# First cross attention of a perceiver block: mask conversion in pieces between rounds, value chunks ahead of key chunks, one copy of the queries in the scratch

## The chip, the cores and the metric

The kernel runs on one core of a Trainium2 chip. The metric is the device time of one execution in microseconds (us); lower is better. Times of before are the median of 3 runs.

## What is computed

The program is a block of six stages, each adding to `x` of shape (2, 256, 256): a cross attention, a convolution and gate layer, a quantised feed-forward layer, a second cross attention, a self attention with heads of 64, and a mixture of experts. The change lies in the first stage alone:

```
q = proj(layernorm(x), Wq, bq); k = proj(ctx, Wk, bk); v = proj(ctx, Wv, bv)   # 16 heads of 16
energy = einsum('bhqd,bhkd->bhqk', q, k) / sqrt(16)
energy = where(mask_input == 0, -1e9, energy)                                  # mask: 256 x 4096, int32
context = einsum('bhqk,bhkd->bhqd', softmax(energy), v)
x = x + context @ Wo.T + bo
```

`x` has 2 batches of 256 queries, `ctx` has 2 batches of 4096 keys of width 256. All is float32.

## The kernel before, in words

`l0_xattn` works through 16 units `u`, each a batch and a pair of heads. Keys are projected in chunks of 512 (`project_k(b, f, j, ct)`, L185: two matmuls for half `f` of the features, a bias on ACT into `kf`, a split into a high part on DVE and a low part on POOL, `split` L174, and two DMAs, L197, into a scratch in DRAM, `KS`). A unit's keys come back from the scratch in another layout (`load_k`, L211, into `kst`, 3 buffers), its queries likewise (`load_q`, L201, from `QS` into `qz`, 4 buffers). Both copies hold a high and a low part of each number, and the queries hold each of them twice. Values are projected in two halves per chunk (`project_v`, L334; a yield after each half), copied on ACT (L351), and stay on chip in `v`.

The main loop (L546) has 8 rounds `g` per unit and two passes `a` per round, one for each head of the pair. Three things run in it, shifted against one another: in unit `u` the scores `st` with queries on the partitions (L388), of which DVE takes the maximum with the mask added (`max_out`, L397, two `st` buffers); ten rounds later the scores `sT` with keys on the partitions and the maximum taken off (`weights_part`: L404 adds a mask with a matmul, L411 the maximum, L421 the scores; exp on ACT L427; POOL multiplies the other half's mask in, L429); and eleven rounds later the sum over values (`weigh`, L437).

So the mask is wanted in two forms. `madd` (queries on the partitions) is made by `make_madd(qc, j, mi)`, L247, one DVE operation for each of 8 pieces and each half `qc` of the queries. `addT` and `keep` (keys on the partitions, L323 and L325) are made from `x0_maskT` in 16 pieces by `make_masks`, which ends with two reductions over `madd` (L328). The raw masks go through the tile `mi` with 3 buffers; the first half's go into `keep`, which is free then.

Work that is not part of the rounds is written as generators in the list `slow`; each pass takes one step of each of them before its own work. `first_batch` gives the rest of the keys and the values of batch 0, `masks` the rest of the masks, `second_batch` (from round 14) the keys of batch 1, `second_values` (from round 68) its values, `project_out` (L460) the output projection of a batch when its last unit is done. Five steps of `first_batch` are taken ahead of the loop: values 0, keys 0 and values 1.

PE, DVE, ACT and POOL execute in the order in which the program writes the instructions (`tc.manual_schedule`, L1236). All DMAs are issued by SP, whose order the scheduler of the framework sets. An engine that waits holds everything behind it. The lines that set the order before the change are

```
for j in range(NJ):
    make_madd(0, j, mis[j])
...
early = first_batch()
for _ in range(5):
    next(early)
slow = [early, masks()]
```

Of the kernel before, what the change touches and what calls it, by code (L numbers as in the profile page):

```python
# [10 lines left out]
F32 = mybir.dt.float32  # L11
# [7 lines left out]
P = 128  # L19
B = 2  # L20
S = 256
NTOK = B * S
# [23 lines left out]
class Kernel:  # L46
# [96 lines left out]
    def l0_xattn(self):  # L143
        nc, T, tc = self.nc, self.T, self.tc
        H, HD, VD, NJ = 16, 16, 17, 8
# [4 lines left out]
        dram = es.enter_context(tc.tile_pool(name="scratch", bufs=1, space=bass.MemoryType.DRAM))  # L150
# [11 lines left out]


        KS = {(b, f): dram.tile([2, P, 2, S2 // 2], F32, name=f"ks{b}{f}") for b in range(B) for f in range(2)}
        QS = [dram.tile([P, 2, 2, NTOK], F32, name=f"qs{f}") for f in range(2)]

        def part_tile(n, early):
            if early:
# [16 lines left out]
        def project_k(b, f, j, ct):  # L185

            ps = self.bank("psK")
            for k in range(2):
                nc.tensor.matmul(  # L189
                    ps, lhsT=w[:, 0, k, f * P : (f + 1) * P], rhs=ct[:, k, :], start=k == 0, stop=k == 1  # L190
                )
            kf = a2.tile([P, 512], F32, name="kf", tag="kf")
            nc.scalar.activation(kf, ps, AF.Identity, bias=bk[:, f : f + 1])
            part = part_tile(512, b + f == 0)
            split(part[:, 0, :], part[:, 1, :], kf)
            for h in range(2):
                nc.sync.dma_start(KS[b, f][h, :, :, j * S : (j + 1) * S], part[:, :, h * S : (h + 1) * S])  # L197

        qz, kst = {}, {}

        def load_q(u):  # L201
            b, hp = divmod(u, NP)
            f, lp = divmod(hp, 4)
            qz[u] = a1.tile([P, 2, S], F32R, name="qz", tag="qz", bufs=4)
            for h in range(2):
                nc.sync.dma_start(
                    qz[u][64 * h : 64 * h + 64].bitcast(F32),
                    QS[f].rearrange("p j i n -> (p j) i n")[64 * lp : 64 * lp + 64, :, b * S : (b + 1) * S],
                )

        def load_k(u, c0, c1):  # L211
            b, hp = divmod(u, NP)
# [9 lines left out]
        cts = [load_ctx(0, 0), load_ctx(0, 1)]  # L222
# [14 lines left out]
        def load_mask(qc, j):  # L237

            mi = a2.tile([P, 2, S], I32, name="mi", tag="mi", bufs=3) if qc else keep[:, j]
            nc.sync.dma_start(  # L240
                mi.rearrange("p a b -> p (a b)"), T["x0_mask"][qc * P : (qc + 1) * P, j * 512 : (j + 1) * 512]
            )
            return mi

        def make_madd(qc, j, mi):
            c, a = divmod(j, 2)
            nc.vector.tensor_scalar(madd[:, qc, c, :, a], mi, 0, -BIG, ALU.is_equal, ALU.mult)  # L247

        mis = []
        self.layernorm(self.xn, self.x)  # L250
        for j in range(NJ):
            project_k(0, 0, j, cts[j])
            if j == 1:
                self.to_T(self.xnT, self.xn)
            if j == 2:
                for f in range(2):
                    ps = self.bank("psQ")
                    for k in range(2):
                        nc.tensor.matmul(
                            ps, lhsT=wq[:, k, f * P : (f + 1) * P], rhs=self.xnT[:, k, :], start=k == 0, stop=k == 1  # L260
                        )
                    qf = a2.tile([P, NTOK], F32, name="qf", tag="kf")

                    nc.vector.tensor_scalar(qf, ps, bq[:, f : f + 1], 0.25, ALU.add, ALU.mult)
                    part = part_tile(NTOK, True)
                    split(part[:, 0, :], part[:, 1, :], qf)
                    for i in range(2):
                        nc.sync.dma_start(QS[f][:, i], part)
            if j == 4:
                load_q(0)  # L270
            if j >= 4:
                mis += [load_mask(0, 2 * (j - 4)), load_mask(0, 2 * (j - 4) + 1)]
            if j in (3, 5, 7):
                load_k(0, j - 3, j - 1)
        load_k(0, 6, 8)
        for j in range(NJ):
            make_madd(0, j, mis[j])

        def rest_of_mask():
            ahead = [load_mask(1, 0), load_mask(1, 1)]  # L280
            for j in range(NJ):
                if j + 2 < NJ:
                    ahead.append(load_mask(1, j + 2))
                yield
                make_madd(1, j, ahead[j])

        bv = a1.tile([P, D], F32, name="bv")
        wo = a1.tile([P, 2, D], F32, name="wo")
# [45 lines left out]
        def project_v(b, j, ct):  # L334

            n = 4 * H * VD
            vf[b, j] = a1.tile([P, n + 16], F32, name="v", tag="v", bufs=9)
            v = vf[b, j][:, :n].rearrange("p (r h s) -> p r h s", r=4, h=H)
            nc.gpsimd.memset(v[:, :, :, HD:VD], 1.0)
            nc.gpsimd.memset(vf[b, j][:, n:], 0.0)  # L340
            for a in range(2):
                ps = self.bank("psV").rearrange("p (r e) -> p r e", r=2)
                for i in range(2):
                    for k in range(2):
                        n0 = (2 * a + i) * P
                        nc.tensor.matmul(  # L346
                            ps[:, i, :], lhsT=ct[:, k, n0 : n0 + P], rhs=w[:, 1, k, :], start=k == 0, stop=k == 1
                        )
                vo, vi = v[:, 2 * a : 2 * a + 2, :, 0:HD], ps.rearrange("p r (h s) -> p r h s", s=HD)
                if b == 0:  # L350
                    nc.scalar.copy(vo, vi)  # L351
                    sum_ctx(b, j, a, ct)
                else:
                    self.evac(vo, vi)
                yield
# [104 lines left out]
        def project_out(b, cxo):  # L460

            cm = self.sm.tile([P, 2], F32, name="cm", tag="cm")
            nc.vector.tensor_reduce(cm, csum[:, b], AX.X, ALU.add)
            nc.vector.tensor_scalar(cm, cm, 1.0 / S2, None, ALU.mult)
            ps = self.bank("psN")[:, 0:D]
            for k in range(2):
                nc.tensor.matmul(
                    ps, lhsT=cm[:, k : k + 1].to_broadcast([P, P]), rhs=w[:, 1, k, :], start=k == 0, stop=k == 1
                )
            mean = a2.tile([P, D], F32, name="mean", tag="mean", bufs=1)  # L470
            nc.scalar.copy(mean, ps)
            yield
            yield
            for qc in range(2):
                t = 2 * b + qc

                cf = cxo[:, qc].rearrange("p h s -> p (h s)")
                nc.vector.scalar_tensor_tensor(cf, mean, none[:, qc : qc + 1], cf, ALU.mult, ALU.add)
                nc.vector.tensor_tensor(cf, cf, bv, ALU.add)
                nc.vector.tensor_tensor(self.x[:, t, :], self.x[:, t, :], bo, ALU.add)  # L480
            yield
            for qc in range(2):
                t = 2 * b + qc
                cf = cxo[:, qc].rearrange("p h s -> p (h s)")
                ps = self.bank("psX")[:, 0:D]
                for k in range(2):
                    nc.tensor.transpose(ps[:, k * P : (k + 1) * P], cf[:, k * P : (k + 1) * P], self.ident)
                cT = a2.tile([P, 2, P], F32, name="cT", tag="cT")
                nc.scalar.copy(cT.rearrange("p a b -> p (a b)"), ps)
                yield  # L490
                yield
                ps = self.bank("psO")[:, 0:D]
                for k in range(2):
                    nc.tensor.matmul(ps, lhsT=cT[:, k, :], rhs=wo[:, k, :], start=k == 0, stop=k == 1)
                nc.vector.tensor_tensor(self.x[:, t, :], self.x[:, t, :], ps, ALU.add)
                yield
# [6 lines left out]
        def chain(gens):  # L503
            for g in gens:
                yield from g
# [4 lines left out]

        def first_batch():

            for j in range(NJ):
                yield from project_v(0, j, cts[j])
                project_k(0, 1, j, cts[j])
                yield

        def second_batch():
# [19 lines left out]
        def masks():  # L538
            yield from rest_of_mask()
            yield from make_masks()  # L540

        early = first_batch()
        for _ in range(5):
            next(early)
        slow = [early, masks()]
        for g in range(8 * NU + 12):  # L546
            u, i = divmod(g, 8)
# [14 lines left out]
            u2, j = divmod(g - 10, 8)  # L562
            u3, j3 = divmod(g - 11, 8)

            for a in range(2):
# [4 lines left out]
                if 0 <= u2 < NU:  # L570
                    p = pt[u2, j, a] = a2.tile([P, 2, 2, S], F32, name="p", tag="p", bufs=5)
                    part = weights_part(qz[u2], kst[u2], msh[u2], a, j, p)
# [766 lines left out]
```

## Time and profile before

| what | before |
|---|---|
| median of 3 runs | 1223.26 us (1222.86 to 1226.22) |
| the profiled execution | 1223.28 us |
| its span, first to last instruction | 1221.5 us |
| busy in the span: PE, DVE, ACT, POOL | 1058.0, 678.3, 461.0, 401.2 us |
| mean granted clock of PE | 0.912 |
| key and query scratch: DMAs L197, L268 | 64 of 256 KB, 4 of 512 KB |
| loads of queries L206, of keys L217 | 32 of 128 KB, 38 |
| last addition to `x` in the stage (L495) starts | 651.69 us |

All times in the stage are us from the first instruction. PE is the tensor engine's matmuls and PEld its weight loads; DVE, ACT and POOL are the vector, scalar and GpSimd engines; SP only issues DMAs. In a line of the timeline come the start, the duration, the engine, the source line, the operation, what it writes and reads, how often, and in square brackets how long the engine had been idle and what released it. In the chain of waits, each line is a piece of the chain that ended last. "Granted clock" is the share of its full clock that PE was given.

### The profile page before, as it was taken

What the parts mean: (1) busy time and instruction counts of PE and PEld (TensorE: products, weight loads), DVE (VectorE), ACT (ScalarE), POOL (GpSimd) and SP (SyncE); (2) the same over time, 40 slices, a digit from 0 to 9 for tenths busy, and PEclk for the clock granted to TensorE, in tenths of its full rate; (3) what the DMA queues carried; (4) which work ended last, traced back from release to release, by engine and by line L of the source; (5) the groups of instructions that cost most, each with busy time, mean ns of one, the idle gap of its engine ahead of it and who ended that gap; (6) DMA issues with size and microseconds to landing.
All of it is one profiled execution on the core that took longest, in us unless ns stands there. A gap on an engine that the chain in (4) does not pass through costs nothing.

```text
span 1221.5 us, 20524 instructions
## 1 busy us (share of the span) xinstructions
PE 1058.0 (87%) x8203; PEld 614.3 (50%) x8204; DVE 678.3 (56%) x1243; ACT 461.0 (38%) x926; POOL 401.2 (33%) x424
## 2 busy tenths in 40 slices
PE   6688899999999899999996595239799889888888
PEld 3354455555566555555553143124466663365666
DVE  3168666666754677777505916974344427557330
ACT  2334466666654456666651210210211212336010
POOL 4114577777763467777760000000000000000000
PEclk9788899999999999999996798558899989979879
DMA  9895044444222211221006623110336440000000
GB/s 320 257 272 176 33 116 113 131 113 117 58 62 70 44 45 46 45 45 36 2 1 226 229 69 99 52 38 27 92 115 194 150 138 0 1 1 1 1 1 18
DMA packets 54446, 108.54 MB, mean 89 GB/s; under 512 B 5568, under 2 KB 27968, under 8 KB 52432
## 3 DMA queue, kind: packets, MB, share of 16 engines
q1 hardware_dynamic: 54352, 107.24, 29.4%
q8 instruction: 64, 1.05, 0.4%
q14 instruction: 30, 0.25, 0.1%
HBM read 87.82 MB, written 19.40 MB: 88 GB/s over the span
## 4 chain that ended last, share of the span: by engine, by line
PE 78%; DVE 13%; issue 3%; ACT 3%; DMA 2%; POOL 1%; SPq 1%; POOLq 0%; ACTq 0%; DVEq 0%
PE av L437 12%; PE st L388 9%; PE sT L421 8%; PE psP L133 7%; PE sT L404 6%; PE psS L909 5%; PE psV L346 4%; PE psK L189 4%; PE av L930 4%; PE ot L1086 2%; DVE yb L687 2%; DVE nm L918 1%; PE psR L999 1%; PE psC L448 1%; PE psI L1209 1%
## 5 line engine op out<-in xcount | busy, mean ns | idle before, releaser
L397 DVE CUSTOM_DVE_ANT_0 junk<-st,madd 128x1024 bf16<-128x1024 f32 x256 | 313.2, 1223 | 113.8 <-PE st L388 112.5
L429 POOL TENSOR_TENSOR p<-p,keep 128x512 int32<-128x512 int32 x256 | 327.7, 1283 | 144.9 <-ACT p L427 138.0
L427 ACT ACTIVATE p<-sT 128x512 f32<-128x512 f32 x512 | 277.9, 595 | 180.7 <-PE sT L421 176.3
L421 PE MATMUL sT<-qz,kst 32*128 32x256 f32 x2048 | 214.2, 326 | 0.0
L388 PE MATMUL st<-kst,qz 32*128 32x512 f32 x1024 | 191.3, 450 | 21.3 <-DVE mx L397 21.3
L100 POOL TENSOR_TENSOR rs<-ve,nhalf 128x4 f32<-128x4 f32 (+1 forms) x12 | 11.1, 928 | 502.1 <-DVE ve L99 502.1
L437 PE MATMUL av<-p,v 128*32 128x256 f32 x2048 | 168.5, 395 | 0.5 <-ACT avs L589 0.5
L421 PEld LDWEIGHTS sT<-qz,kst 32*128 32x128 f32 x2048 | 161.2, 189 | 0.7
L388 PEld LDWEIGHTS st<-kst,qz 32*128 32x128 f32 x1024 | 78.1, 186 | 96.6 <-issue 64.9
L411 PE MATMUL sT<-msh,oneb 3*128 3x512 bf16 x512 | 103.8, 388 | 0.0
L404 PE MATMUL sT<-addT,identb 128*128 128x512 bf16 x256 | 99.9, 390 | 0.0
L189 PE MATMUL psK<-ctx,wkv 128*128 128x512 f32 x128 | 65.0, 639 | 7.2 <-DMA ctx<-in_ctxT 7.2
L176 POOL TENSOR_TENSOR part<-kf,part 128x512 f32<-128x512 f32 x32 | 41.6, 1301 | 84.3 <-DVE part L175 75.6
L404 PEld LDWEIGHTS <-identb 128*128 128x128 bf16 x256 | 25.9, 101 | 84.8 <-issue 84.2
L346 PE MATMUL psV<-wkv,ctx 128*128 128x256 f32 x256 | 64.5, 397 | 0.0
L909 PE MATMUL psS<-w,qk 128*128 128x512 f32 x128 | 62.4, 622 | 0.0
L437 PEld LDWEIGHTS av<-p,v 128*32 128x32 f32 x2048 | 42.3, 108 | 37.5 <-POOL p L429 1.4
L912 DVE SCALAR_TENSOR_TENSOR sc<-psS,sb,w 128x512 f32<-128x512 f32 x32 | 24.0, 751 | 66.3 <-PE psS L909 66.3
L930 PE MATMUL av<-w,pT 128*128 128x256 f32 x256 | 59.8, 380 | 0.0
L346 PEld LDWEIGHTS psV<-wkv,ctx 128*128 128x128 f32 x256 | 47.4, 194 | 17.7 <-issue 11.8
L88 ACT COPY pT<-psT 128x512 f32<-128x512 f32 (+2 forms) x24 | 16.7, 696 | 100.9 <-PE psT L938 92.1
L930 PEld LDWEIGHTS av<-w,pT 128*128 128x128 f32 x256 | 46.7, 191 | 5.2
(258 smaller groups left out, 1289.5 us busy)
## 6 DMA issues: line engine op xcount, KB each, us to landing
ks<-part SPq DMA_DIRECT2D x64, 256.0 KB, 2.9
kst<-ks SPq DMA_DIRECT2D x30, 512.0 KB, 6.6
ctx<-in_ctxT SPq DMA_DIRECT2D x24, 512.0 KB, 5.4
w<-in_ctxT SPq DMA_DIRECT2D x16, 512.0 KB, 7.2
w<-in_ctx SPq DMA_DIRECT2D x16, 512.0 KB, 3.7
w<-in_m_w SPq DMA_DIRECT2D x16, 512.0 KB, 4.2
qz<-qs SPq DMA_DIRECT2D x32, 128.0 KB, 6.5
mi<-in_x_maskT SPq DMA_DIRECT2D x16, 256.0 KB, 3.7
```

The lines of the kernel that those rows point to most:

```text
L189: nc.tensor.matmul(ps, lhsT=w[:, 0, k, f * P : (f + 1) * P], rhs=ct[:, k, :], start=k == 0, stop=k == 1)
L346: nc.tensor.matmul(ps[:, i, :], lhsT=ct[:, k, n0 : n0 + P], rhs=w[:, 1, k, :], start=k == 0, stop=k == 1)
L388: nc.tensor.matmul(st[:, h, :], lhsT=qz[r : r + 32, i, qc * P : (qc + 1) * P], rhs=kst[r : r + 32, c * 512 : (c + 1) * 512], start=i == 0, ...
L397: nc.vector.tensor_tensor_reduce(out=junk, in0=st, in1=madd[:, qc, c].rearrange("p h a k -> p h (a k)"), scale=1.0, scalar=-1e38, op0=ALU. ...
L404: nc.tensor.matmul(sts[0], lhsT=self.identb, rhs=addT[:, j].rearrange("p a q -> p (a q)"), start=True, stop=False, skip_group_check=True,)
L411: nc.tensor.matmul(sts[h], lhsT=oneb[r : r + 3, :], rhs=msh[r : r + 3, :].unsqueeze(1).to_broadcast([3, 2, S]), start=h >= NADD, stop=Fals ...
L421: nc.tensor.matmul(sts[h][:, a * S : (a + 1) * S], lhsT=kst[r : r + 32, n0 : n0 + P], rhs=qz[r : r + 32, i, :], start=False, stop=i == 1, ...
L427: nc.scalar.activation(p[:, h].rearrange("p a q -> p (a q)"), sts[h], AF.Exp)
L429: nc.gpsimd.tensor_tensor(p[:, 1].bitcast(I32), p[:, 1].bitcast(I32), keep[:, j], ALU.mult)
L437: nc.tensor.matmul(av[c : c + 32, :], lhsT=vf[:, o : o + 32], rhs=p[:, h, a, :], start=j == 0 and par == 0, stop=j == NJ - 1, tile_positio ...
L909: nc.tensor.matmul(ps, lhsT=qk[:, k, t * P : (t + 1) * P], rhs=ctxT[kb][:, k, :], start=k == 0, stop=k == 1)
L930: nc.tensor.matmul(av, lhsT=pT[:, c, :], rhs=cn[i][:, c, :], start=i + c == 0, stop=i == 7 and c == 3)
```

## The change

The masks: before the loop only the first two pieces of the first half are converted; the generator `rest_of_mask` converts one piece per step, first the other six of that half, then the eight of the second half, whose loads it asks for four steps ahead. The tasks: four chunks of values (eight steps) are made ahead of the loop instead of five steps of values and keys by turns; in the loop a key chunk and half a value chunk take turns. The queries: `QS` holds each number once, written by one DMA per half, and `load_q` reads it by four DMAs, each of which doubles its rows by a source with a step of 0. `project_out`: two empty steps stand behind each of its six DVE operations on the context and on `x`.

```diff
-        QS = [dram.tile([P, 2, 2, NTOK], F32, name=f"qs{f}") for f in range(2)]
+        QS = [dram.tile([P, 2, NTOK], F32, name=f"qs{f}") for f in range(2)]
...
             for h in range(2):
-                nc.sync.dma_start(
-                    qz[u][64 * h : 64 * h + 64].bitcast(F32),
-                    QS[f].rearrange("p j i n -> (p j) i n")[64 * lp : 64 * lp + 64, :, b * S : (b + 1) * S],
-                )
+                for i in range(2):
+                    nc.sync.dma_start(
+                        qz[u][64 * h : 64 * h + 64, i].bitcast(F32),
+                        QS[f][32 * lp : 32 * lp + 32, i, b * S : (b + 1) * S].unsqueeze(1).to_broadcast([32, 2, S]),
+                    )
...
-                    for i in range(2):
-                        nc.sync.dma_start(QS[f][:, i], part)
+                    nc.sync.dma_start(QS[f], part)
...
-        for j in range(NJ):
+        for j in range(2):
             make_madd(0, j, mis[j])
 
         def rest_of_mask():
-            ahead = [load_mask(1, 0), load_mask(1, 1)]
-            for j in range(NJ):
-                if j + 2 < NJ:
-                    ahead.append(load_mask(1, j + 2))
-                yield
-                make_madd(1, j, ahead[j])
+            ahead = []
+            for j in range(2, 2 * NJ):
+                if j >= 4 and len(ahead) < NJ:
+                    ahead.append(load_mask(1, len(ahead)))
+                if j < NJ:
+                    make_madd(0, j, mis[j])
+                else:
+                    make_madd(1, j - NJ, ahead[j - NJ])
+                yield
...
                 nc.vector.scalar_tensor_tensor(cf, mean, none[:, qc : qc + 1], cf, ALU.mult, ALU.add)
+                yield
+                yield
                 nc.vector.tensor_tensor(cf, cf, bv, ALU.add)
+                yield
+                yield
                 nc.vector.tensor_tensor(self.x[:, t, :], self.x[:, t, :], bo, ALU.add)
-            yield
+                yield
+                yield
...
         def first_batch():
 
+            for j in range(NJ // 2):
+                yield from project_v(0, j, cts[j])
+            rest = chain([project_v(0, j, cts[j]) for j in range(NJ // 2, NJ)])
             for j in range(NJ):
-                yield from project_v(0, j, cts[j])
                 project_k(0, 1, j, cts[j])
                 yield
+                next(rest)
+                yield
...
-        for _ in range(5):
+        for _ in range(8):
             next(early)
```

## Prediction

> **What bounds the kernel now.** I read the slice rows of the page first: only there does one see which stretches are not bound by the tensor engine. In these rows a slice is 30.5 us and a digit is tenths.
>
> ```profile
> PE   6688899999999899999996595239799889888888
> PEclk9788899999999999999996798558899989979879
> DMA  9895044444222211221006623110336440000000
> ```
>
> The first cross attention is slices 0 to 20. From slice 5 on PE is full at full clock, except slice 13; slices 0 to 4 are not. The stages after slice 21 wait for `x`, which the first stage ends by writing, so what that stage gains or loses moves them as a whole. Second view: busy time in stretches of 5 us (columns: PE, PEld, DVE, ACT, POOL busy, granted clock, DMA share, GB/s).
>
> ```profile
> 40.00:45.00 5.00, 5.00 (x24) 3.32 (x24) 0.87 (x3) 1.90 (x4) 0.00 (x0) 1.00 1.07 349
> 45.00:50.00 5.00, 0.55 (x3) 0.15 (x1) 2.38 (x9) 1.21 (x3) 0.33 (x1) 0.78 0.68 197
> 50.00:55.00 5.00, 3.89 (x8) 1.68 (x8) 1.06 (x2) 0.00 (x0) 2.55 (x6) 0.50 0.50 154
> 55.00:60.00 5.00, 1.04 (x2) 0.00 (x0) 0.00 (x0) 0.69 (x1) 0.00 (x0) 0.50 0.94 217
> 60.00:65.00 5.00, 0.86 (x4) 0.50 (x4) 2.48 (x5) 0.00 (x0) 0.00 (x0) 0.50 0.90 302
> ```
>
> From 45 to 65 us PE is busy 6.3 us of 20, no other engine does more, and most of these matmuls run at half the clock. Third view, the timeline there, says who waits.
>
> ```profile
> 48.46 0.43 DVE L247 TENSOR_SCALAR madd<-keep 128x512 bf16<-128x512 int32 x1 [0.42 <-DMA keep<-in_x_mask]
> 49.67 1.37 POOL L176 TENSOR_TENSOR part<-kf,part 128x512 f32<-128x512 f32 x1 [16.86 <-DVE part L175]
> 51.11 1.22 PE L388 MATMUL st<-kst,qz 32*128 32x512 f32 x4 [5.56 <-DVE mx L397]
> 55.61 2.34 SPq L240 DMA_DIRECT2D mi<-in_x_mask  x3
> 62.52 0.43 DVE L247 TENSOR_SCALAR madd<-mi 128x512 bf16<-128x512 int32 x1 [11.46 <-DMA mi<-in_x_mask]
> 64.14 1.22 PE L388 MATMUL st<-kst,qz 32*128 32x512 f32 x4 [8.10 <-DVE mx L397]
> ```
>
> It is one chain. DVE works in program order and stands at eight conversions L247, each of which needs its mask (the last runs at 48.46). Behind them on DVE is the split L175 of the key task, so POOL idles 16.86 us, the scratch write that SP must issue waits for POOL, and the masks of the second half of the queries stand behind that write on SP: issued at 55.61, used at 62.52. The maximum L397 waits for those, and PE, with two `st` buffers, for the maximum. Fourth view, the chain of work that ended last, after that stall:
>
> ```profile
> 77.16 1.93 PE psV L346 x8
> 79.08 0.66 PE st L388 x4
> 79.74 1.91 PE psK L189 x4
> 81.66 0.66 PE st L388 x4
> ```
>
> Here a pass (one turn of the loop over `a`, two to a round) is 1.92 + 0.66 = 2.58 us and PE-bound, be its task half a value chunk or a key chunk.
>
> **The change, part by part.** The profiled execution took 1223.28 us, its span 1221.5; the median of the runs is 1223.26, so the sum made on the profile needs no correction.
>
> (1) Masks by pieces, values ahead: until the loop. PE is continuous from 14.6 to 45.5 us in the trace. A value chunk takes 33.34 - 29.89 = 3.45 us and a key chunk 1.72 (33.34 to 35.06). Four chunks of values from 29.89 end at 29.89 + 4 x 3.45 = 43.7, and the loop starts. Its first `st` comes at 45.4; key scratch and queries for it were there at 40.3, when that matmul ran before. On DVE only two conversions precede it, whose masks had landed at 36.4 and 37.1; the other six have passes 1 to 6, and their masks were there by 48.5, where pass 6 begins at 43.7 + 5 x 2.58 = 56.6. So DVE reaches the split when the key chunk is ready, and the chain of above has no first link.
>
> (2) Passes 1 to 16 hold 8 key chunks and 8 half value chunks (before: 19 passes, five tasks ahead). DVE has 1.30 (L397) + 0.34 (one conversion, from its start to the next start) + half of 0.35 (L175) = 1.8 us per pass, less than 2.58: PE-bound, 16 x 2.58 = 41.3, to 85.0.
>
> (3) Passes 17 to 20 lose their filler: before, three of them had tasks. `st` alone is 0.66 of PE, so DVE sets the pace: 1.48 us from maximum to maximum with a conversion between (106.40, 107.88, 109.36 in the timeline). 4 x 1.48 = 5.9: pass 21, the first with weights, starts at 90.9 instead of 106.38 (first L404). Gain **15.5**.
>
> (4) Conversions last to pass 30 (before: 24). While POOL masks `p`, these DVE operations took 0.81 to 0.95 us instead of 0.42, ending 0.3 us after POOL's. A DVE pass is then 1.30 + 0.34 plus what it waits, so between 1.64 and 2.1 (112.49 to 114.42 is 1.93), against 1.70 of PE at full clock (116.37 to 118.07). For the six added passes: 0 to 2.4; I take nearer the lower end, since a DVE pass that starts behind POOL's operation fits in 1.70: **-1**.
>
> (5) The clock. Passes 21 to 24 took 10.0 us before, at granted clock 0.50. The Trainium skill ("TensorE: Matmul & The Clock Gate", section on what is actually happening) throttles after an idle window of about 3.4 us and releases after a busy one. The trace agrees on the step (clock low from 109.4 to 116.0, 6.6 us, then full to 122.9), not on the condition: from 105.80 to 109.20 PE was busy 2.20 of 3.40, with no gap over 0.91, and it still dropped. By the page's rule passes 17 to 20, whose gaps would be 0.8, keep full clock and passes 21 to 24 take 4 x 1.70 = 6.8: 3.2 more gain. By the row, 45% busy is less than the 65% that sufficed to drop it. I follow the row: the same dip, **0**.
>
> (6) The two reductions L328 (4.41 us each on DVE) come six passes later, in passes 31 and 32. Their stall of PE stays; but now the first key chunk of batch 1 (pass 32 in both) lies beside it. Before it was on the path, at 136.68 for 1.82 us. Between 0 and +1.8; DVE gets its 0.4 us of L175: **+1.5**.
>
> (7) Steps between the operations of `project_out`. For batch 0 the six DVE operations stand together, 420.39 to 424.8, two of them 1.39 and 1.51 us long, and PE loses 0.85 (transposes L487 waiting for L479) and 1.29 (`st` at 426.06 waiting for L397). Spread over 12 passes, each has DVE's slack of 1.70 - 1.30 per pass and the lead of two `st` buffers. Between 0 and 2.1: **+2**. For batch 1 nothing lies beside it, so the order is as before: 0.
>
> (8) Queries once in the scratch: 2 writes of 512 KB less on queues that are full (DMA share 1.07), 4 issues of 64 KB per unit instead of 2 of 128 KB. SP issues almost without a pause from 24.5 to 47.5; load_q(0) adds 2 x 0.60, the writes take away 2 x 0.40. The skill speaks against the split ("DMA: Bandwidth & Descriptors", rules for kernel authors: coalesce; under 64 KB mostly overhead). If small transfers doubled the landing (median 6.5 us in the trace), the first queries would land at 30.9 + 13 = 43.9, by the row at about 40; both before 45.4, and later units are loaded a unit ahead: 0 by either, and if that cover were gone, 1.2 us once. The writes removed: 0, as PE bounds that stretch.
>
> (9) The added wait: masks of the second half are asked for four passes ahead with three buffers, so the fourth waits on SP for the conversion of the first, with scratch writes and key loads behind it. Those have two passes (`part`) or a unit as lead. The masks keep three passes, 7.7 us; they landed in 3.3 to 6.9. For the transposed masks in passes 17 to 20 three passes are 4.4 us against landings of 2.7 to 6.2 (median 3.7). 0 to 2: **-0.5**.
>
> Sum: 15.5 - 1 + 1.5 + 2 - 0.5 = 17.5. 1223.3 - 17.5 = **1205.8 us**.
>
> **Rivals.**
> *The masks' landing becomes the new wait.* For: the queues are 0.9 busy in this stretch in the trace, and three buffers now have to carry 16 transposed masks at 1.5 to 1.7 us a pass. At the longest landing seen anywhere here for masks, 6.9, plus 0.4 to issue and 0.34 to convert, three passes take 7.6 us: 2.55 a pass, harmless in passes 7 to 14, but +0.85 to 1.05 in passes 17 to 30, 13 us in all. Against: in passes 20 to 24 of the trace the same three buffers ran at 1.5 to 2 us with no idle DVE. It would give 1205.8 + 13 = 1219.
> *Slower.* The same ring at pass 17 to 30, but stalling more than is gained: 17.5 / 14 = 1.25 us a pass over its pace of 1.7, so a landing above 3 x 2.95 - 0.75 = 8.1 us each time. The weights' first L404 needs `addT` five passes after its conversion (before: eleven), so it would be held too. With landings of 9.1 (the longest of the key loads) it gives 3.3 a pass, 14 x 1.6 = 22 lost: about 1228. Against: no mask load landed so late.
> *The change does not remove the stall*: if SP kept the second half's masks behind the scratch writes and those behind DVE, the 45 to 65 us hole would only move by a few passes, and (7) alone would be gained; about 1221. Against: the first link, eight conversions ahead of the split, is gone from DVE's order itself.
>
> **How the numbers follow.** Likeliest case 0.84 (1200 to 1213: without (6) and (7) 1209, with 2 more for (4) and (9) 1213; with the rule of (5) and all of the upper ends 1201). Landing rival 0.08, hole remains 0.04, slower 0.04. A run can tell about 0.3% (3.7 us). Faster by more than that 0.92, within 0.04, slower 0.04. The range keeps to the likeliest case's bounds, 1200 to 1213.
>
> **What would show it.** After: PE full between 40 and 85 us at clock 1.00; key and value matmuls alternating with `st`; no L247 on DVE before which it waits over 2 us; first L404 at about 91; a dip of clock near 90 to 97; the two L328 one after the other with psK between them; no idle PE near the project_out of batch 0. Wrong if L247, L323 or L325 wait for DMA in many passes, or if L404 still starts after 100.

## The result and the profile after

The changed kernel takes 1206.13 us, the median of 4 runs (1204.17 to 1207.56), against 1223.3 for the kernel before on the same chip: a ratio of 0.9854, 95% interval 0.9832 to 0.9875. The forecast was 1205.8. The profiled execution of after took 1204.17 us, with a span of 1202.4 us and a mean granted clock of 0.919; it is the fastest of its four, so it flatters the change by about 2 us. Every time and ratio in this document is of runs in the fast state; only three runs of e1, of its twelve, were in the slow one (1236 to 1237 us at a granted clock of 0.895).

The slice rows of the page after (40 slices of 30.1 us, counted from 0, digits in tenths):

```profile
PE   7998899999999999999987594248899889888888
PEclk9998899999999999999997797559899989889879
DMA  8895344333233012220008323111335430000000
```

PE is now full in slices 1 and 2 too. What is left in the first stage are slices 3 and 4, 90 to 150 us. The busy time in stretches of 5 us (PE, PEld, DVE, ACT, POOL, granted clock, DMA share, GB/s) answers to the second view of before:

```profile
45.00:50.00 5.00, 5.00 (x21) 2.71 (x20) 3.57 (x7) 1.90 (x4) 1.55 (x3) 1.00 0.71 219
50.00:55.00 5.00, 5.00 (x21) 2.71 (x20) 3.47 (x7) 1.89 (x4) 1.38 (x1) 1.00 0.94 213
55.00:60.00 5.00, 5.00 (x21) 2.71 (x20) 2.27 (x5) 1.90 (x4) 1.55 (x3) 1.00 0.92 316
60.00:65.00 5.00, 5.00 (x21) 2.62 (x20) 4.50 (x9) 1.90 (x4) 1.38 (x1) 1.00 0.80 219
```

The hole, with 6.3 us of PE work in 20 us, is gone: 20 of 20, at full clock. In the timeline of DVE the split now stands ahead of the conversions instead of behind eight of them:

```profile
46.10 0.43 DVE L175 TENSOR_SCALAR part<-kf 128x512 int32<-128x512 int32 x1 [8.84 <-ACT kf L193]
46.44 0.42 DVE L248 TENSOR_SCALAR madd<-keep 128x512 bf16<-128x512 int32 x1
46.77 1.22 DVE L400 CUSTOM_DVE_ANT_0 junk<-st,madd 128x1024 bf16<-128x1024 f32 x1
```

(The code's lines have moved: L397 is L400 here, L404 L407, L323 and L325 are L326 and L328, L328 is L331.) Two passes to a round, the passes can be counted, and their starts on PE tell where time was won and lost:

| start of pass | before | after | gain so far |
|---|---|---|---|
| 21, the first with weights | 106.38 | 90.16 | 16.2 |
| 25 | 116.37 | 100.45 | 15.9 |
| 30 | 133.29 | 108.90 | (not comparable: the long reductions stand in passes 25 and 26 before, in 31 and 32 after) |
| 31 | 134.98 | 112.17 | (the same) |
| 36 | 147.56 | 133.20 | 14.4 |
| 157, ahead of `project_out` of batch 0 | 419.84 | 405.52 | 14.3 |
| 221 | 538.08 | 521.64 | 16.4 |
| 276, the last | 635.05 | 618.63 | 16.4 |

So 16.2 us are won before pass 21, 1.9 are given back by pass 36, and 2.1 come with `project_out`. The span gained 19.1: another 2.7 lie in the stages behind, in this one execution. Below, "from pass 21 to pass 36" means from the start of the one to the start of the other.

### The profile page after: what moved, and what is told of

Read it like the earlier page. It is cut to its first block, busy times and chain, and to the rows that moved or that the text cites. A ratio compares the mean times of both kernels' runs of the same rounds, so it can differ in the third digit from the quotient of the medians.

```text
span 1202.4 us, 20561 instructions
## 1 busy us (share of the span) xinstructions
PE 1053.4 (88%) x8204; PEld 612.4 (51%) x8204; DVE 676.9 (56%) x1243; ACT 461.2 (38%) x926; POOL 401.9 (33%) x424
## 4 chain that ended last, share of the span: by engine, by line
PE 80%; DVE 12%; ACT 3%; DMA 3%; issue 1%; POOL 1%; SPq 0%; POOLq 0%; ACTq 0%; DVEq 0%
PE av L440 12%; PE st L391 9%; PE sT L424 8%; PE psP L133 7%; PE sT L407 6%; PE psV L349 5%; PE psS L921 5%; PE psK L189 5%; PE av L942 4%; PE ot L1098 2%; DVE yb L699 2%; DVE nm L930 1%; PE psR L1011 1%; PE psC L451 1%; PE psI L1221 1%
## 5 line engine op out<-in xcount | busy, mean ns | idle before, releaser
L400 DVE CUSTOM_DVE_ANT_0 junk<-st,madd 128x1024 bf16<-128x1024 f32 x256 | 313.1, 1223 | 105.9 <-PE st L391 104.5
L407 PE MATMUL sT<-addT,identb 128*128 128x512 bf16 x256 | 100.3, 392 | 0.0
L407 PEld LDWEIGHTS <-identb 128*128 128x128 bf16 x256 | 25.9, 101 | 85.1 <-issue 84.6
L349 PE MATMUL psV<-wkv,ctx 128*128 128x256 f32 x256 | 61.8, 389 | 0.0
```

Source lines behind the costliest of these rows:

```text
L349: nc.tensor.matmul(ps[:, i, :], lhsT=ct[:, k, n0 : n0 + P], rhs=w[:, 1, k, :], start=k == 0, stop=k == 1)
L400: nc.vector.tensor_tensor_reduce(out=junk, in0=st, in1=madd[:, qc, c].rearrange("p h a k -> p h (a k)"), scale=1.0, scalar=-1e38, op0=ALU. ...
L407: nc.tensor.matmul(sts[0], lhsT=self.identb, rhs=addT[:, j].rearrange("p a q -> p (a q)"), start=True, stop=False, skip_group_check=True,)
```

## The experiments

Each kernel is the changed one with the edit shown, and each time is a median with its ratio to before, timed on the same chip. In the forecasts on record, "pass" counts as above. One thing has to be taken out when profiles are compared: in those of e1, e5, e6, e7 and e8 the clock was low for 3.4 to 6.8 us between 14 and 22 us, ahead of the work that these edits change, and the loop starts 2.0 to 3.8 us later than in after (first `st` at 47.25 to 48.97, against 45.21).

**e1: the mask part undone.** The task order, the scratch and `project_out` stay as changed.

```diff
-        for j in range(2):
+        for j in range(NJ):
             make_madd(0, j, mis[j])
...
+            ahead = [load_mask(1, 0), load_mask(1, 1)]
+            for j in range(NJ):
+                if j + 2 < NJ:
+                    ahead.append(load_mask(1, j + 2))
                 yield
+                make_madd(1, j, ahead[j])
```

> The changed kernel with the mask part undone: all eight pieces of the first half converted ahead of the loop, the second half's from pass 2 on, two loads ahead. Task order, query scratch and project_out as changed. Theory A (the hole from 45 to 65 us comes from DVE's program order: conversions ahead of the split, and the second half's masks wanted while they stand behind the scratch writes on SP): the split of the first key chunk in the loop waits for the last mask (48.5 us), the second half's masks are issued at 52 to 55 and land near 61, PE stands for about 9 us; first L404 at about 99 instead of 90.2, total near 1215. Theory B (the order of the tasks filled the hole): no hole, total as the changed kernel, 1206.

Measured: 1219.09 us, 0.9943 (0.9926 to 0.9960); pass 21 at 104.22. By the ratios (0.9943 against 0.9854) the mask part is worth about 11 of the 18 us. The profile agrees: from the first `st` (47.95) to pass 21 it takes 56.3 us, in after 45.0. DVE in e1:

```profile
50.94 0.36 DVE L175 TENSOR_SCALAR part<-kf 128x512 int32<-128x512 int32 x1
60.87 0.43 DVE L248 TENSOR_SCALAR madd<-mi 128x512 bf16<-128x512 int32 x1 [8.43 <-DMA mi<-in_x_mask]
```

and SP's queue and PE there:

```profile
52.77 1.22 SPq L197 DMA_DIRECT2D ks<-part  x2
54.05 2.34 SPq L241 DMA_DIRECT2D mi<-in_x_mask  x3
62.49 1.22 PE L388 MATMUL st<-kst,qz 32*128 32x512 f32 x4 [6.72 <-DVE mx L397]
```

It is the chain of before, with values ahead of it: split, scratch write, then the masks behind that write, used 6.8 us after their issue, and PE behind the maximum.

**e2: only the first half ahead.** All eight conversions of the first half stand ahead of the loop again, the second half's stay as changed: asked for four steps ahead, from pass 7 on.

```diff
-        for j in range(2):
+        for j in range(NJ):
             make_madd(0, j, mis[j])
...
-                if j < NJ:
-                    make_madd(0, j, mis[j])
-                else:
+                if j >= NJ:
                     make_madd(1, j - NJ, ahead[j - NJ])
```

> The changed kernel, only the first half's eight conversions put back ahead of the loop; the second half's stay in passes 7 to 14. It tells the two links of theory A apart. If the early demand for the second half's masks is the costly link: DVE reaches the first split at 48.8 instead of 46.1, at most 2 us of PE idle before pass 3, first L404 at 90 to 92, total 1206 to 1209. If the eight conversions ahead are the costly link by themselves: a hole of 8 us or more, total over 1213.

Measured: 1210.25 us, 0.9872 (0.9842 to 0.9902), an interval that overlaps that of after; pass 21 at 90.67, 0.5 us later than after. DVE reaches the split only at 49.33 (after: 46.10), yet PE waits only this:

```profile
50.88 0.72 PE L389 MATMUL st<-kst,qz 32*128 32x512 f32 x4 [0.20 <-DVE mx L398]
```

So the eight conversions ahead of the split, which the prediction called the first link, cost 0.5 us by themselves once nothing hangs on the split at once. The other 11 us (e1 less e2, from the first `st` to pass 21) come from the second half's masks being wanted from pass 2 while their loads stand behind the scratch write. The two are links of one chain, and cutting the second is nearly enough; cutting the first alone was not tried.

**e3: the old task order** (values and keys by turns, five steps ahead of the loop), with the new masks.

```diff
-            for j in range(NJ // 2):
-                yield from project_v(0, j, cts[j])
-            rest = chain([project_v(0, j, cts[j]) for j in range(NJ // 2, NJ)])
             for j in range(NJ):
+                yield from project_v(0, j, cts[j])
                 project_k(0, 1, j, cts[j])
                 yield
-                next(rest)
-                yield
...
-        for _ in range(8):
+        for _ in range(5):
```

> The changed kernel with the task order undone: values and keys of a chunk after each other, five steps ahead of the loop. Masks by pieces as changed. Theory A: the loop starts at 38.5, every mask is there when its pass comes (landings 36.4 to 48.5), 19 passes of 2.58 us end at 87.5, one pass of 1.48, first L404 at about 89; total 1205 within 2. Theory B: the hole is back in large part, total over 1215.

Measured: 1207.85 us, 0.9843 (0.9802 to 0.9884); pass 21 at 89.95 against 90.16. With the new masks, the order of the tasks is worth nothing that can be measured. (With the old ones it may be worth something: e1, which has the new order, is still 0.57% or 7 us faster than before, and `project_out` explains 2.1 of them; the rest was not taken apart.)

**e4: the query scratch as before** (each number twice, two loads of 128 KB).

```diff
-                    nc.sync.dma_start(QS[f], part)
+                    for i in range(2):
+                        nc.sync.dma_start(QS[f][:, i], part)
```

> The changed kernel with the query scratch undone: four writes of 512 KB instead of two, two loads per unit instead of four. Theory A (these transfers lie under PE): no PE idle comes or goes before 90 us, first L404 within 0.3 us of 90.2, total 1206 within 1.5. Theory C (the gain is relief of the DMA queues by 1 MB): the first keys and masks land 3 us later, total near 1209.

Measured: 1207.26 us, 0.9849 (0.9815 to 0.9883), pass 21 at 90.16 in both. Nothing.

**e8: `project_out` without the empty steps.**

```diff
                 nc.vector.tensor_tensor(cf, cf, bv, ALU.add)
-                yield
-                yield
                 nc.vector.tensor_tensor(self.x[:, t, :], self.x[:, t, :], bo, ALU.add)
-                yield
-                yield
+            yield
```

> The changed kernel with the empty steps of project_out taken out. Passes 21 to 150 as the changed kernel; at the end of batch 0 (passes 157 to 173) PE stands again, 0.85 for the transposes and 1.29 for the maximum: 2.1 us later from pass 173 on, total about 1208. If DVE had had the slack for them together: no difference.

Measured: 1211.02 us, 0.9877 (0.9857 to 0.9898). From pass 157 to pass 221 it takes 118.24 us, as in before, against 116.12 in after: the steps are worth 2.12. The rest of the difference lies where the code is the same in both: 2.1 us ahead of pass 21 (the low clock before the loop) and 3.1 from pass 21 to pass 36 (46.2 against 43.0 us).

**e10: the changed kernel once more**, to see how far such a difference goes without any edit.

> The changed kernel again, nothing edited, beside e9 and e11 on the same chip: total 1206 within 2. If the lengths of the low clock in passes 21 to 36 come by chance, these passes differ from the first profile (22.0 us for passes 21 to 30, 21.0 for 31 to 35) by up to 3 us each.

Measured: 1206.25 us (1204.99 to 1210.49), 0.9850 (0.9830 to 0.9870). The profile caught the slowest of its five runs, 1210.49, so the profiles of after (its fastest run) and e10 bracket the kernel. From pass 21 to pass 36 it took 47.1 us there, 4.1 more than in after, and the stages behind were only 0.3 us shorter than in before.

**e5: the wait for the transposed masks taken away.** The `keep` pieces are loaded into `keep` itself and converted in place, so `mi` has to carry 8 pieces instead of 16.

```diff
-                mi = a2.tile([P, 2, S], I32, name="mi", tag="mi", bufs=3)
+                mi = keep[:, j] if h else a2.tile([P, 2, S], I32, name="mi", tag="mi", bufs=3)
```

> The changed kernel; the eight transposed masks for `keep` are loaded into `keep` itself and converted there, so only the eight for `addT` go through the three buffers of `mi`. Theory A (the term for the landing was set too small: the last two masks held DVE for 0.76 and 1.53 us and this went on to the reductions): waits of DVE for transposed masks fall from 3.5 us to under 0.5, pass 31 starts 1.5 to 2.3 us earlier, total about 1204.5. Rival (DVE is late there because it waits for POOL, not for the masks): no change, 1206.

Measured: 1204.09 us, 0.9820 (0.9798 to 0.9842), an interval that just overlaps that of after, so a gain in the whole is likely but not shown. No conversion waits for a transposed mask any more (in after: 3.6 us in all). Pass 30 takes 1.69 us, against 3.27 in after; what that shows is weighed further down.

**e6: the reductions over `madd` in 16 pieces**, one in every second pass (and a small one over their results).

```diff
+            tops = a1.tile([P, 2, 8], F32, name="tops")
+            for n in range(16):
+                qc, m = divmod(n, 8)
+                c, h = divmod(m, 2)
                 nc.vector.tensor_reduce(
-                    none[:, qc : qc + 1], madd[:, qc].rearrange("p c h a k -> p (c h a k)"), AX.X, ALU.max
+                    tops[:, qc, m : m + 1], madd[:, qc, c, h].rearrange("p a k -> p (a k)"), AX.X, ALU.max
                 )
                 yield
+                yield
+            nc.vector.tensor_reduce(none, tops, AX.X, ALU.max)
```

> The changed kernel; the two reductions of 4.41 us over `madd` are cut into 16 of 512 columns, one in every second pass, with a small one at the end. If the two reductions cost PE 8.8 us of standing and of low clock (passes 31 to 36: 21.0 us for 12.2 us of work): about 8 gained, total about 1198, and the clock stays full after 101 us. If the pieces (about 0.6 us each, with a pass of 1.30 on DVE against 1.69 on PE) make DVE the bound instead: half of it, about 1202.

Measured: 1200.99 us, 0.9788 (0.9764 to 0.9813). By the ratios that is 8 us less than the changed kernel, by the medians 5. From pass 31 to pass 36 it took 12.55 us, in after 21.03. The group's line (count, shortest, median and longest in ns, first and last start), and then five microseconds of after's reductions and ten of e6's pieces:

```profile
L334 DVE TENSOR_REDUCE tops<-madd x16: 673/682/684, 117.9 to 181.6; 128x1 f32<-128x512 bf16 x16
```

```profile
115.00:120.00 5.00, 2.76 (x26) 1.04 (x25) 5.00 (x4) 1.78 (x3) 0.95 (x1) 1.00 0.00 0
```

```profile
115.00:120.00 5.00, 5.00 (x52) 2.41 (x50) 4.74 (x9) 2.83 (x5) 3.56 (x3) 1.00 0.02 5
120.00:125.00 5.00, 5.00 (x73) 2.68 (x69) 4.74 (x10) 3.89 (x9) 4.09 (x8) 1.00 0.32 105
```

**e7: e5 and e6 together**, **e11: the same with the old task order**, **e9: e7 with the keys of batch 1 from round 7 instead of 14**, so that PE has tasks beside the scores in passes 17 to 30.

```diff
-            if g == 14:
+            if g == 7:
                 slow.append(second_batch())
```

> Both edits. If they are separate losses they add: about 1196.5. If the masks' waits only mattered because the reductions came right behind them, as e6: about 1198.

> Both edits of e7 with the task order of before. By theory A the order of the tasks is worth nothing: the same as e7, about 1198. With one pass without filler instead of four the clock may stay full longer: up to 2 us less.

> Both edits of e7, and the keys of batch 1 from round 7 on instead of 14. It tests the terms of the prediction for passes 17 to 30 (DVE sets the pace, PE is idle and its clock falls): two to three key chunks of 1.82 us then lie beside DVE's work, and PE is busy 75% instead of 45% in passes 17 to 20. If idle PE is what drops the clock: it stays at full, or is low for one stretch of 3.4 us instead of two or three; with the chunks 4 to 7 us less than e7 to pass 41, total about 1193. If the drop does not depend on the filler: about 3 us less, 1195. If the loads of the context now delay the masks: no gain, 1198.

Measured: e7 1197.90 us, 0.9765 (0.9744 to 0.9785); e11 1196.36, 0.9756 (0.9728 to 0.9783); e9 1194.42, 0.9749 (0.9733 to 0.9765), the lowest median. The three intervals overlap one another, and e7's overlaps e6's: whether e5's gain adds to e6's, and whether e9 gains on e7, the times alone don't tell. e7 and e11 show once more that the order of the tasks is worth nothing. In e9, from pass 36 to pass 141 it takes 3.8 us less than in e7 (218.1 against 221.9), since the tasks of that PE-bound stretch are partly done; from pass 21 to pass 36 it takes 1.9 more, as they lie there.

## Why the prediction was right, and where its terms were not

The total was right, and so was the mechanism of the hole, which carries most of it. But the four terms that lie between passes 21 and 36 were forecast to cancel and didn't, most of all that of the clock; that the sum came out all the same is partly luck.

**(1) to (3), the hole: right.** The first `psK` of the loop starts at 43.40 (forecast 43.7), the first `st` at 45.21 (45.4), a pass takes 2.58, and the first weights come at 90.16 (90.9). The gain was 16.2 where the sum has 15.5. What e2 corrects is the emphasis: not the conversions ahead of the split, but the second half's masks behind the scratch write, carry the price. That the values ahead matter, which the sum's first step used to place the loop's start, holds only for that place: with the old task order (e3) pass 21 starts at the same time, because both orders have the same PE work ahead of it.

**(4) to (6) and (9) together: forecast 0, measured -1.9 in after and -1.7 to -6.2 in five other profiles.** In after, e10, e4, e3, e2 and e8, PE, DVE, ACT and POOL run the same instructions from pass 21 to pass 36 (SP's order of loads differs between some of them); e5 is set beside them. The passes, and the time in them for which the clock was low:

| us | 21 to 25 | 25 to 30 | low clock there | 30 to 31 | 31 to 36 | low clock there | 21 to 36 |
|---|---|---|---|---|---|---|---|
| before | 9.99 | 16.92 (with the reductions) | 10.2 | 1.69 | 12.58 | 0 | 41.18 |
| after | 10.29 | 8.45 | 0 | 3.27 | 21.03 (with the reductions, as all below) | 10.2 | 43.04 |
| e10 | 11.84 | 9.07 | 1.4 | 3.76 | 22.45 | 15.6 | 47.12 |
| e4 | 11.72 | 10.43 | 4.6 | 1.69 | 19.08 | 6.8 | 42.92 |
| e3 | 12.53 | 11.65 | 7.5 | 1.69 | 21.46 | 10.2 | 47.33 |
| e2 | 11.33 | 10.41 | 4.6 | 1.69 | 22.89 | 13.4 | 46.32 |
| e8 | 11.33 | 11.69 | 7.5 | 1.69 | 21.47 | 10.2 | 46.18 |
| e5 | 9.37 | 8.45 | 0 | 1.69 | 19.06 | 6.8 | 38.57 |

*(4), conversions until pass 30: 0 instead of -1.* At full clock the five passes from 25 on take 1.69 each, PE's own pace (after, e5). Where they take longer, they do so by 0.43 us for each us of low clock (1.98 for 4.6 in e4, 3.20 for 7.5 in e3), so that is term (5). (The last transposed mask is converted in pass 31, before in pass 25: one later than the prediction counts, and six apart as it says.)

*(5), the clock: mis-sized, the largest miss in most of the profiles.* The prediction followed the row of before (a drop at 45% busy) against the rule of the Trainium skill ("TensorE: Matmul & The Clock Gate", what is actually happening), which by its idle window would have kept the clock up. It dropped, from 86.8 on, with PE far from idle, but stayed low for 13.7 us and not for 6.8:

```profile
85.00:90.00 5.00, 3.20 (x14) 1.42 (x14) 4.77 (x11) 0.60 (x3) 1.20 (x5) 0.68 0.96 266
90.00:95.00 5.00, 4.80 (x36) 2.75 (x35) 3.91 (x9) 1.62 (x4) 1.29 (x1) 0.50 0.99 341
95.00:100.00 5.00, 5.00 (x45) 2.94 (x45) 4.83 (x8) 2.11 (x5) 2.55 (x2) 0.50 0.63 215
```

In after that costs only 0.3 us up to pass 25, since it ends there. In e4, e3 and e2 it lasted 17.1 us and in e8 20.5, and up to pass 30 these took 3.3 to 5.7 us more than before's 9.99 + 5 x 1.69; masks that came late up to pass 25 may have a part in that. In e10 the clock fell again at 113.6, and PE did pass 31 with its key chunk at half speed:

```profile
115.00:120.00 5.00, 5.00 (x26) 2.56 (x26) 5.00 (x4) 1.09 (x3) 2.55 (x2) 0.50 0.00 0
```

*(9), the masks' landing: mis-sized in after, 1.6 us instead of 0.5.* The transposed masks were late six times in after, together 3.6 us of DVE's time; the last one shows on PE, as pass 30 is 1.6 us longer:

```profile
105.23 0.99 DVE L328 TENSOR_SCALAR keep<-mi 128x512 int32<-128x512 int32 x1 [0.76 <-DMA mi<-in_x_maskT]
108.89 0.71 DVE L326 TENSOR_SCALAR addT<-mi 128x512 bf16<-128x512 int32 x1 [1.53 <-DMA mi<-in_x_maskT]
```

In e10 that last wait was longer, and so was pass 30:

```profile
110.85 0.88 DVE L326 TENSOR_SCALAR addT<-mi 128x512 bf16<-128x512 int32 x1 [2.58 <-DMA mi<-in_x_maskT]
```

The prediction compared landings with three passes of lead. It left out what shares the queues there: three loads of `ctx` of 512 KB and those of the next queries, issued between 92 and 102 us. Two of them stand right ahead of that last mask on SP:

```profile
100.47 0.60 SPq L160 DMA_DIRECT2D ctx<-in_ctxT  x1
101.81 0.58 SPq L160 DMA_DIRECT2D ctx<-in_ctxT  x1
102.48 7.48 SPq L316 DMA_DIRECT2D mi<-in_x_maskT  x4
```

Issued at 102.48, it landed 6.4 us later. In e4, where SP issued these loads of `ctx` at 94.67 and 97.13, the same mask landed 2.7 us after its issue, and pass 30 took 1.69. It did so in e3, e2 and e8 as well, so e5's 1.69 doesn't show by itself that its edit took the wait off PE. The first rival's mechanism was real, in two profiles of six, at an eighth to a sixth of its price of 13 us.

*(6), the key chunk beside the reductions: 0 instead of +1.5 in after.* The stall that the reductions make is 16.92 - 5 x 1.69 = 8.5 us in before, and 21.03 - 12.55 (the same passes in e6) = 8.5 in after. DVE and PE there in after:

```profile
114.49 4.41 DVE L331 TENSOR_REDUCE none<-madd 128x1 f32<-128x4096 bf16 x1
119.96 4.41 DVE L331 TENSOR_REDUCE none<-madd 128x1 f32<-128x4096 bf16 x1
```

```profile
113.87 1.98 PE L189 MATMUL psK<-ctx,wkv 128*128 128x512 f32 x4
120.09 0.57 PE L391 MATMUL st<-kst,qz 32*128 32x512 f32 x2 [2.33 <-DVE mx L400]
125.89 0.79 PE L391 MATMUL st<-kst,qz 32*128 32x512 f32 x2 [3.28 <-DVE mx L400]
```

The key chunk does lie beside the reductions, as said. But the stall goes with the low clock in it: 6.5 us in e4 and e5, where the clock was low for 6.8; 8.5 to 8.9 in after, e3 and e8, where it was low for 10.2; 10.3 in e2 (13.4) and 9.9 in e10 (15.6). So 2 us were saved, as the term says, in two of the seven profiles. DVE's lateness from (9) alone doesn't decide it: the first reduction starts 2.3 us after pass 31 in after, but 0.9 after it in e3 and e8 as well as in e4 and e5.

So a difference of 4 us between executions of the same instructions goes with the clock; which causes which these runs don't separate. PE's waits come before a drop, and a low clock delays PE. For a term of 1 us, then, one profile says little here; it takes several, and intervals between passes in each.

**(7) right: 2.12** (e8) for a forecast of 2. **(8) right: 0** (e4). The rule against small transfers ("DMA: Bandwidth & Descriptors", rules for kernel authors) didn't bite at 64 KB, where its bound stands: the query loads landed in 6.1 us (median) where those of 128 KB took 6.5, and they are asked for a unit ahead.

**The sum, done again.** 16.2 up to pass 21, -1.7 to -6.2 from there to pass 36, 2.1 for `project_out`: at the last pass after is 16.4 ahead of before, e4 16.5, e10 and e3 12.5. The medians differ by 17.2. Behind the last pass, where all run the same instructions, after's profile has 2.7 us less than before's and e10's 0.3. That too goes with the clock: it was low there for 177.5 us in before and in e10, and for 170.7 in after. For after's profile the terms give: the hole 0.7 more and the conversions 1 less cost than in the sum, the key chunk 1.5 less, the masks' landing 1.1 more cost and the clock 0.3: 17.5 + 0.7 + 1 - 1.5 - 1.1 - 0.3 = 16.3, and with the stages behind the 19.1 of this execution. The spans of e4, e10 and e3 are 16.4, 12.8 and 9.8 shorter than before's (the last two are the slowest runs of their kernels). That the median meets the forecast within 0.3 us is therefore luck; that it comes within a few us is the hole.

**The other two rivals fell.** No mask was late enough to lose what had been gained, and the hole didn't move; e1 shows what "the hole remains" looks like, at 1219.09.

## What to carry to other kernels

An engine that runs in program order and a DMA queue that runs in issue order make one chain when work waits for a load that is queued behind a store which waits for that engine: find it by following one wait through every queue it passes, then ask for the load ahead of the store, a few steps before it is used. When a stall is removed, the next passes show what had been hidden in it: here the ring of masks and the two long reductions, which, spread in pieces of 0.68 us, gave 5 to 8 us more (e6). And in a stretch where the clock drops, terms of 1 or 2 us can't be added one by one: the same instructions took 42.9 us in one execution and 47.3 in another.

## What the runs showed of the hardware

In the first 200 us of the 13 profiles the clock was low in 31 stretches, each a multiple of about 3.41 us long: 3.4, 6.8, 10.2, 13.7, 17.1 and 20.5 us were seen. In the 3.41 us ahead of each of them PE was busy for 0.55 to 2.50 us, and in the last 3.41 us of each it was busy throughout. So it can drop with PE up to 73% busy (e11, at 94.28). In e9, with tasks put into those passes, PE was 76% busy from 85 to 90 us (the first line), but only 61% in the 3.41 us ahead of the drop at 90.8 (the second), which then lasted 6.8 us:

```profile
85.00:90.00 5.00, 3.82 (x18) 1.52 (x18) 5.00 (x12) 2.15 (x6) 2.47 (x6) 1.00 0.90 277
87.40:90.81 3.41, 2.09 (x13) 0.80 (x11) 3.41 (x8) 1.20 (x4) 1.87 (x4) 1.00 0.71 247
```

At what share it stays up is not settled: in e10 it did so past 3.41 us of which PE was busy for 2.10, and dropped after the next 3.41, with 2.06.

A DVE conversion of 128x512 integers takes 0.42 us alone. Of those of the transposed masks, 49 in the 13 profiles started while POOL multiplied masks into `p`: they took up to 1.5 us (0.99 and 0.71 in the two lines above of after), and each ended 0.28 to 0.38 us behind POOL's operation.
